# Moving one Gelu of three behind other transposes, one row's norm ahead of the next row's statistics, and twenty transposes of the identity at the start

## The chip, the cores and the metric

The kernel runs as one program on one NeuronCore of a Trainium2 chip. TensorE (PE) multiplies and transposes, VectorE (DVE) and ScalarE (ACT) read PSUM and work elementwise, GpSimd (POOL) works on SBUF and issues indirect DMAs, and SyncE (SP) issues most other DMAs. Each engine runs its own list of instructions strictly in order; a semaphore wait at the head of a list holds up everything behind it. The metric is the device time of one execution in microseconds (us); the median of several executions is compared.

## The reference

Eight rows of 512 tokens of width 128 go through two layers in float32. A layer norms its input (mean and variance, no gain), and adds an attention and a feed-forward part to it.

- Layer 0: attention with 16 heads of width 64 and a causal softmax; beside it a mixture of 32 experts of which each token uses six, plus a shared expert.
- Layer 1: attention with four heads of width 32 (queries and keys normalised to length one, two key-value heads, gate on the result). Beside it three residual blocks, each of which does this:

```python
y = _qlora_linear(h, qweights[i0], ...)   # 128 -> 128
y = _layernorm(y, ln_gamma[blk], ln_beta[blk])
y = jax.nn.gelu(y, approximate=False)
y = _qlora_linear(y, qweights[i1], ...)
h = y + h
```

## The kernel before, in words

The order of all instructions on every engine is written out by hand (`manual_schedule`): the Python code calls small functions one after the other, and each call appends its instructions to the engines' lists. Nothing reorders them later.

**The start.** Eight loads bring the rows `x_0` to `x_7` on SP's queue, while ACT's queue loads the projection weights. POOL builds the identity `ident` (used as one operand of every transpose) and the masks. A row is normed by the generator `normed(b)` in four steps: (1) statistics of its four tiles on DVE (L187, L188), one `isq` on DVE (L150) and one power on POOL (`rstd`, L153); (2) four subtract-multiply instructions on DVE (`xe`, L195); (3) four transposes on PE into a PSUM bank (`tp`, L202); (4) the copy out of PSUM, `xnT`, on ACT or DVE. `ln(0, 1, 0, 0, 0)` at L1129 takes step 1 of row 0, step 1 of row 1, and then steps 2, 3, 4 of row 0. After that come the first projections (L427), the first scores (L457) and the first value projections (L438).

**Layer 0** is a loop over 193 ticks, three per pair of heads. A tick computes scores for the next third, exponentials for this one, transposes of the last one (`pt_ps`, L501) and, once per pair, the product with the values. Places in a tick (0 to 3) take side work: the deque `steps` (rest of the norms, routing, weights of layer 1; `fill` takes steps from it until a credit of DVE time is spent), the experts and the indirect gathers of the experts' results into the row (L697, on POOL).

**Layer 1** is a loop over units `u = 3 r + k`; a slot `r` is three units (k = 0, 1, 2) and works on attention row `r`, while the three feed-forward blocks n = 0, 1, 2 work on rows r + 2, r + 1 and r (`of_slot`). In unit k, `second_layer` issues: the second linear of the blocks of the last slot (`summed`, L1050; only k = 1), the output projection (`z`, k = 2), a first linear for block k (`lin_ps`, L1008), the scores of the next unit (`sc`, L915, then `neg`, L923, on DVE), this unit's exponentials on ACT (L937), `norm` of block k (squares on DVE L1024, `lin_rstd` and `yn` on POOL), the transposes and Gelu of all three blocks of the last slot (`yn_ps` L1040 on PE, L1041 on ACT; only k = 0), the product with the values (`y_ps`, k = 1), the transposes of the last unit's probabilities (`pt_ps`, L956), and the transposes of the divisors that POOL has spread out (`wide`, `tp`, L826; only k = 0). Steps of the next row's preparation (`prepared`) stand at fixed places between them. In the last slots there are no more rows for blocks 0 and 1, so that only block 2 is left in slot 8's unit 0.

PSUM has banks in three rings: two "s", two "t" and four "m". The first linear, half of layer 1's scores, `yn_ps`, `tp` and `o_ps` all take the next "m" bank, and wait until the engine that read its last content is done. `evacuate` chooses between DVE and ACT by two running sums of estimated load.

## Time and profile before

| | |
|---|---|
| median of four runs | 1172.28 us (1171.77 to 1177.32) |
| the profiled execution's own time | 1174.18 us |
| its span, first to last instruction | 1172.5 us |
| PE busy | 1082.3 us, 92% |
| DVE busy | 759.5 us, 65% |
| ACT busy | 742.0 us, 63% |
| POOL busy | 682.0 us, 58% |
| mean granted clock of PE | 0.984 |

The profile is of one execution. "Busy" is a share over stages that have different limits, so a stage must be read by itself. A timeline row gives start, duration, engine, source line, operation, what it writes and reads, and in square brackets how long the engine stood idle before it and what ended that. PEld is the loading of PE's stationary operand. The granted clock (PEclk) is 1.00 at full speed and 0.50 when PE is throttled to half; the record of the clock begins with its first event at 17.66 us, and 1.00 is shown ahead of that for want of a record.

### The profile page before, as it was taken

To read this page: it belongs to the slowest core of one execution; us is meant where nothing else is said; L and a number is where in the kernel's file an instruction comes from. 1 tells how busy PE (TensorE), PEld (TensorE's weight loads), DVE (VectorE), ACT (ScalarE), POOL (GpSimd) and SP (SyncE) were. 2 spreads that over 40 slices of the span, in tenths; PEclk is the share of its full clock that TensorE was granted. 3 is DMA by queue.
4 is the path that set the end of the run, shared out by engine and by line. 5 is a ranking of instruction groups with operands and counts; after the bars stand their busy time and mean duration, and the time that the engine had idled before them with its cause. 6 is when DMAs were issued, how large, how long until landed. Compare 5 with 4: busy or idle time off the path is not lost.

```text
span 1172.5 us, 25274 instructions
## 1 busy us (share of the span) xinstructions
PE 1082.3 (92%) x8534; PEld 727.8 (62%) x8534; DVE 759.5 (65%) x2563; ACT 742.0 (63%) x1977; POOL 682.0 (58%) x738
## 2 busy tenths in 40 slices
PE   5899999999999999999999999999995978888986
PEld 2556556566766686667676766565663555655664
DVE  4676775665566646664666566766751667778884
ACT  3478685666466646674667466646652656887785
POOL 2008888888840000288888600488888788776650
PEclk9999999999999999999999999999997998999999
DMA  9807943368875766699889864322322241000000
GB/s 287 223 2 212 264 135 101 124 180 260 235 206 160 203 175 163 168 228 205 198 198 230 198 162 117 90 26 35 74 52 30 25 97 15 10 10 10 10 20 18
DMA packets 204052, 151.05 MB, mean 129 GB/s; under 512 B 17682, under 2 KB 192276, under 8 KB 203924
## 3 DMA queue, kind: packets, MB, share of 16 engines
q1 hardware_dynamic: 166340, 119.51, 37.2%
q0 software_dynamic: 36864, 28.34, 13.0%
q10 hardware_dynamic: 720, 1.61, 0.4%
q8 instruction: 67, 1.10, 0.4%
q14 instruction: 61, 0.50, 0.1%
HBM read 93.52 MB, written 55.87 MB: 127 GB/s over the span
## 4 chain that ended last, share of the span: by engine, by line
PE 59%; POOL 18%; DVE 9%; issue 6%; DMA 4%; SPq 2%; ACT 1%; ACTq 0%; DVEq 0%; POOLq 0%
PE sc L457 10%; POOL x L697 10%; PE pt_ps L501 9%; PE yps L524 9%; PE qk_ps L427 7%; PE z L585 4%; PE v_ps L438 3%; POOL rn L153 3%; PE ye_ps L679 2%; PE u_ps L667 2%; PE g_ps L667 2%; PE xt_ps L655 2%; DMA rb<-sums 1%; DVE neg L923 1%; POOL xs L605 1%
## 5 line engine op out<-in xcount | busy, mean ns | idle before, releaser
L697 POOL DMA_INDIRECT x<-ys,index x192 | 300.6, 1565 | 276.2 <-DMA ys<-yg 149.1
L480 ACT ACTIVATE neg<-neg,nmax 128x512 f32<-128x512 f32 (+3 forms) x512 | 281.3, 554 | 22.4 <-DVE nmax L465 22.2
L465 DVE CUSTOM_DVE_ANT_0 neg<-sc,mask 128x512 f32<-128x512 f32 (+3 forms) x512 | 225.0, 486 | 93.7 <-PE sc L457 88.6
L169 ACT COPY pT<-pt_ps 128x512 f32<-128x512 f32 x283 | 155.7, 583 | 141.3 <-PE pt_ps L501 123.8
L457 PE MATMUL sc<-qkT 64*128 64x384 f32 (+3 forms) x1024 | 193.3, 465 | 21.2 <-DVE nmax L465 21.1
L605 POOL DMA_INDIRECT xs<-xe,index x192 | 187.4, 976 | 36.7 <-issue 36.2
L501 PEld LDWEIGHTS pt_ps<-ident,neg 128*128 128x128 f32 x1280 | 137.6, 141 | 74.7 <-issue 33.8
L501 PE MATMUL pt_ps<-ident,neg 128*128 128x128 f32 x1280 | 182.5, 282 | 1.3 <-DVE pT L163 1.0
L524 PEld LDWEIGHTS yps<-pT,vs 128*64 128x64 f32 x1792 | 110.5, 137 | 77.3 <-issue 22.7
L457 PEld LDWEIGHTS sc<-qkT 64*128 64x128 f32 x1024 | 87.0, 187 | 114.6 <-DVE nmax L465 36.5
L524 PE MATMUL yps<-pT,vs 128*64 128x128 f32 (+1 forms) x1792 | 153.8, 323 | 0.8 <-ACT pT L169 0.8
L480 ACT ACTIVATION_READ_ACCUMULATOR neg<-neg,nmax 128x1 f32 x512 | 97.8, 191 | 0.0
L163 DVE COPY pT<-pt_ps 128x512 f32<-128x512 f32 x117 | 76.8, 685 | 7.6 <-PE pt_ps L501 4.1
L561 DVE TENSOR_TENSOR yT<-yT,rb 128x512 f32<-128x512 f32 x64 | 46.4, 732 | 49.2 <-DMA rb<-sums 49.1
L169 ACT COPY yT<-yps 128x512 f32<-128x512 f32 x42 | 24.6, 586 | 80.3 <-PE yps L524 80.3
L937 ACT ACTIVATE neg<-neg,nmax 128x512 f32<-128x512 f32 (+3 forms) x128 | 70.2, 552 | 0.1
L427 PE MATMUL qk_ps<-xnT,wk_sb 128*128 128x512 f32 x128 | 68.4, 617 | 0.0
L427 PE MATMUL qk_ps<-xnT,wq_sb 128*128 128x512 f32 x128 | 67.2, 607 | 0.8 <-ACT xnT L169 0.7
L438 PE MATMUL v_ps<-wv_sb,xnT 128*128 128x512 f32 x128 | 65.4, 596 | 0.0
L585 PE MATMUL z<-wz_sb,yT 128*128 128x128 f32 x512 | 63.5, 276 | 1.4 <-DVE yT L561 1.0
L585 PEld LDWEIGHTS z<-wz_sb,yT 128*128 128x128 f32 x512 | 60.5, 192 | 5.0 <-issue 2.1
L153 POOL TENSOR_TENSOR lin_rstd<-isq,neg_half 128x4 f32<-128x4 f32 x24 | 26.9, 1120 | 61.2 <-DVE isq L150 48.8
(198 smaller groups left out, 1706.4 us busy)
## 6 DMA issues: line engine op xcount, KB each, us to landing
wx<-in_experts SPq DMA_DIRECT2D x256, 128.0 KB
xs<-zero SPq DMA_DIRECT2D x16, 1280.0 KB
xg<-xs SPq DMA_DIRECT2D x64, 320.0 KB
rb<-sums SPq DMA_DIRECT2D x128, 128.0 KB
ys<-yg SPq DMA_DIRECT2D x32, 512.0 KB
oh<-slot_rows SPq DMA_DIRECT2D x32, 128.0 KB
xs<-xe,index POOLq DMA_INDIRECT x192
x<-ys,index POOLq DMA_INDIRECT x192
```

Of the source, the lines that this page charges most:

```text
L163: nc.vector.tensor_copy(dst, src)
L169: nc.scalar.copy(dst, src)
L427: nc.tensor.matmul(ps, lhsT=w[:, c * P : (c + 1) * P], rhs=xnT[b], start=True, stop=True)
L438: nc.tensor.matmul(ps, lhsT=xnT[b][:, t * P : (t + 1) * P], rhs=wv[:, g * 512 : (g + 1) * 512], start=True, stop=True,)
L457: nc.tensor.matmul(sc[j][:, off : off + w], lhsT=qT[r, i * P : (i + 1) * P], rhs=kT[r, :w], start=True, stop=True,)
L465: nc.vector.tensor_tensor_reduce(out=neg[:, j, off : off + w], in0=sc[j][:, off : off + w], in1=mask[:, L - w :], scale=-1.0, scalar=HUGE, ...
L480: nc.scalar.activation(neg[:, j, off : off + w], neg[:, j, off : off + w], AF.Exp, bias=nmax[:, 2 * k + j : 2 * k + j + 1], scale=-1.0, ac ...
L501: nc.tensor.transpose(ps[:, (start + k) * P : (start + k + 1) * P], pr[:, j, k * P : (k + 1) * P], ident,)
L524: nc.tensor.matmul(y[j * DK0 : (j + 1) * DK0, i * P : (i + hi - lo) * P], lhsT=vs[:, k, h * DK0 : (h + 1) * DK0], rhs=pt[:, j, lo:hi, :].r ...
L585: nc.tensor.matmul(z[:, t, :], lhsT=yts[b * NPAIR + c][:, (NT - 1 - t) * P : (NT - t) * P], rhs=wz[:, c, :], start=(c == 0), stop=False,)
L605: move = nc.gpsimd.indirect_dma_start(xs[h], bass.IndirectOffsetOnAxis(index[:, t, k : k + 1], 0), xe[h][:, t % TH, :], None,).ins
L697: nc.gpsimd.indirect_dma_start(x_b[b][:, tb, :], None, ys[t // TH], bass.IndirectOffsetOnAxis(index[:, t, k : k + 1], 0), compute_op=ALU.add,)
```

## The change

1. In unit k = 0 of a slot, the transposes and the Gelu of block 2 are no longer issued with those of blocks 0 and 1, but behind the transposes of the probabilities and of the divisors. This concerns eight slots (rows 0 to 7 of block 2). Around it, on ACT, the copies of the probabilities and the divisors now come ahead of that Gelu, and since the Gelu's estimated load is added later, `evacuate` gives a few copies to the other engine.
2. At the start row 0 goes through all its steps before row 1's statistics are taken. In the deque the steps of rows 1 to 3 are ordered anew to fit: row 1's second step comes ahead of row 2's statistics; the logits of the router (L223) come one half tick earlier on PE, ahead of a scores group.
3. Ahead of all that PE does twenty transposes of `ident` into a bank of its own, whose content nobody reads.

The instructions of POOL and SP stay as they are, in number and in order; PE gets the twenty transposes, and ACT and DVE the same work with a few copies exchanged.

```diff
     steps = deque(
-        ln(2, 1, 3, 1, 1, 2, 2, 2, 3, 3, 3) + [routes[0]] * 8 + [scaled] + [routes[0]] * 13
+        ln(1, 2, 1, 1, 3, 2, 2, 2, 3, 3, 3) + [routes[0]] * 8 + [scaled] + [routes[0]] * 13
...
         job(new, norm, *item)
         if k == 0:
             for old in of_slot(r - 1):
-                job(True, gelu, *old)
+                job(old[0] < 2, gelu, *old)
         job(k == 1 and past, values1, r - 1)
         advance(1)
         job(0 <= u - 1 < 3 * B, transposes1, *divmod(u - 1, 3))
         job(k == 0 and past, spread1, r - 1)
+        if k == 0:
+            for old in of_slot(r - 1):
+                job(old[0] == 2, gelu, *old)
         job(k == 2 and past, stored, r - 1)
...
-    for step in ln(0, 1, 0, 0, 0):
+    warm = bank("m", "warm")
+    for _ in range(20):
+        nc.tensor.transpose(warm[:, :P], ident, ident)
+    for step in ln(0, 0, 0, 0, 1):
         take(step)
```

## The prediction

> **What bounds the kernel now.** I read the chain of waits on the page first, then the timeline of the first 60 us, then the granted clock by stretches, then the timeline of every place in layer 1 where block 2's transposes stand.

> ```profile
> PE 59%; POOL 18%; DVE 9%; issue 6%; DMA 4%; SPq 2%; ACT 1%; ACTq 0%; DVEq 0%; POOLq 0%
> ```

> The chain is PE's, but for short stretches, from 13 to about 760 us. From there to 994 us the gathers on POOL set the pace, and they start when the ticks of layer 0 allow it. So a start that comes earlier carries through to 994 us; POOL and SP keep their order. From 994 us on DVE, POOL and PE take turns. The start:

> ```profile
> 7.14 0.17 DVE L150 TENSOR_SCALAR isq<-mv 128x4 f32<-128x4 f32 x1
> ...
> 7.40 1.05 POOL L153 TENSOR_TENSOR rstd<-isq,neg_half 128x4 f32<-128x4 f32 x1 [3.37 <-DVE isq L150]
> 9.21 0.29 DVE L187 BATCH_NORM_STATS2 bn<-x 128x6 f32<-128x128 f32 x1 [1.90 <-DMA x<-in_x]
> ...
> 11.01 1.11 DVE L195 TENSOR_SCALAR xe<-x,mv,rstd 128x128 f32<-128x128 f32 x4
> ...
> 13.33 2.08 PE L427 MATMUL qk_ps<-xnT,wq_sb 128*128 128x512 f32 x2 [0.67 <-ACT xnT L169]
> ...
> 16.91 1.41 PE L427 MATMUL qk_ps<-xnT,wq_sb 128*128 128x512 f32 x2
> ```

> Row 0's `rstd` is ready at 8.45, but `xe` stands behind row 1's statistics, which wait for row 1's load until 9.21. The first projections take 1.87 and 1.71 us from start to start, against 0.86 later: PE is at half speed here, until 17.66. The clock by stretches (columns: stretch, length, busy PE, PEld, DVE, ACT, POOL, then granted clock, DMA share, GB/s):

> ```profile
> 14.25:17.66 3.41, 3.41 (x5) 1.35 (x4) 0.69 (x1) 0.51 (x1) 0.00 (x0) 1.00 1.14 355
> 51.79:55.21 3.42, 1.13 (x6) 0.71 (x7) 3.35 (x21) 2.31 (x6) 0.00 (x0) 1.00 0.48 130
> 55.21:58.62 3.41, 3.41 (x11) 1.73 (x8) 3.19 (x31) 1.02 (x3) 0.13 (x1) 0.50 0.00 0
> 898.30:901.71 3.41, 3.20 (x11) 2.30 (x12) 1.55 (x7) 1.52 (x4) 2.99 (x2) 0.50 0.16 19
> 901.71:905.12 3.41, 3.41 (x11) 1.43 (x11) 1.38 (x7) 0.58 (x1) 2.92 (x2) 0.50 0.35 43
> ```

> ```profile
> 1040.44 0.63 PE L1040 MATMUL yn_ps<-ident,yn 128*128 128x128 f32 x4 [1.43 <-DVE nmax L923]
> ...
> 1042.24 0.17 DVE L150 TENSOR_SCALAR isq<-lin_s 128x4 f32<-128x4 f32 x1
> ...
> 1042.49 1.02 POOL L153 TENSOR_TENSOR lin_rstd<-isq,neg_half 128x4 f32<-128x4 f32 x1 [3.30 <-DVE isq L150]
> ```

> Block 2's transposes wait 1.43 us for a bank, which DVE frees by reading scores. But DVE has no gap from 1035.0 to 1047.7, and what follows is POOL: `lin_rstd`, `yn`, `rn` to 1048.75, then DVE again. The wait is PE's alone. The last slot:

> ```profile
> 1158.73 0.66 PE L1040 MATMUL yn_ps<-ident,yn 128*128 128x128 f32 x4 [0.56 <-POOL yn L1031]
> 1158.98 0.24 DVE L969 RECIPROCAL rinv<-ssum 128x16 f32<-128x16 f32 x1
> ...
> 1159.36 0.61 POOL L971 COPY wide<-rinv 128x512 f32<-128x512 f32 x1 [0.68 <-DVE rinv L969]
> 1159.46 1.28 ACT L1041 ACT_TABLE_LOAD   x1 [2.43 <-PE yn_ps L1040]
> 1160.10 0.60 PE L826 MATMUL tp<-ident,wide 128*128 128x128 f32 x4
> ...
> 1161.59 1.13 PE L1050 MATMUL o_ps<-yn,wT 128*128 128x512 f32 x2 [0.89 <-ACT yn L1041]
> ```

> Here everything hangs on block 2's Gelu: its transposes, the table load and Gelu (to 1161.54), `o_ps`, the values, the end. The divisors' `tp` can start only at 1160.0.

> **The change part by part.**

> *Row 0 first.* `xe` can start at 8.45 + 0.05 = 8.50 and ends 9.61 (1.11 as now). The last transpose ends at about 9.93 (0.04 + 0.28), the copy at 10.57 (0.58 + 0.06 of gaps), the first projection starts at 10.6 instead of 13.33: -2.7. Its weights landed by 7.15, the keys' by 11.45 at the latest (SP's load that waits for their lane was issued then); they are needed at about 12.4. Row 1's statistics (1.9) follow at 9.6 to 11.5 and lie ahead of the first `qkT` copy, which can't start before 12.4: hidden, as long as PE is at half speed; at full speed the copy would wait 0.1.

> *The clock.* In the profiled run PE's unbroken work began at 13.33 and full speed came 4.33 later, so half of that, 2.2 us, was lost. From 10.6 on the clock comes back 3.41 to 6.83 later, as the grid falls: 1.7 to 3.4 lost, 2.6 in the middle: +0.4 against this run.

> *Twenty transposes.* At half speed eight transposes took 1.70 us from start to start (980.23 to 981.93), 0.21 each; twenty from 1.4 us, when `ident` is there, end at about 5.7. PE has nothing else until 8.9, so they cost nothing; they would cost if each took over 0.37. Gain: between 0 and -2.5 (the 2.2 lost above and 0.3 of the first `tp`). I take 0. To wake the clock a stretch of the grid must lie wholly in 4.25 us, which holds for (4.25 - 3.41) / 3.41 = 25% of positions, and then 3.2 us without work follow: the row at 51.79 lost the clock with a gap of 3.06.

> [...]

> *Rows 1 to 3 in new order.* The same DVE instructions between 25 and 35 us; one copy of `vs` (0.69) comes onto DVE, one `qkT` and one `pT` leave it. The logits (3.69 on PE) run ahead of 0.63 of scores instead of behind. PE then waits for DVE anyway (3.06 at 54.08). I take +0.2, with ends -0.6 (one `tp` that no longer stands in the way) and +0.9 (0.44 of transposes behind a wait, 0.4 of scores). Start in all: -2.7 + 0.4 + 0.2 = -2.1.

> *Block 2's Gelu, slots 1 to 5* (979 to 1097 us). PE fills its 1.43 with the probabilities' transposes (0.87), waits for the same bank with `tp`, then does `yn_ps`: `o_ps` starts about 0.5 earlier. ACT loses its gap of 0.39 and starts the exponentials 0.2 earlier. DVE and POOL, on which the slot hangs, wait for none of it: 0. Ends: -1.43 for each of five, -7.2, if PE did bind; +0.6 each, one ACT copy ahead of the Gelu, +3.0.

> *Slot 6* (1121.58, waited 1.30): from here the chain is PE's to 1139. `o_ps` starts at 1122.7 instead of 1123.36: -0.6.

> *Slot 7* (1142.54). `tp` waits for `wide` until 1143.03, `yn_ps` follows to 1144.1. On ACT the table load ends at 1143.46; then one Gelu (0.73), two `pT` copies and `rT` (0.55 each), and only then the second Gelu, done at 1146.6 instead of 1144.9. `o_ps` of block 2 ends 1.2 later. ACT's exponentials, 0.7 late, and the values' 1.2 catch up in the waits for `pT`: z starts 0.8 late. +0.8.

> *Slot 8* (the fence above). The probabilities' transposes go first, then PE waits for `wide` (1159.97) with `tp` at 1160.0, and `yn_ps` runs 1160.5 to 1161.1 instead of 1158.73 to 1159.40. The table load stands behind it as now: +1.7 on everything behind. What is late next is `o_ps`, the values, the end; nothing covers it.

> End in all: -0.6 + 0.8 + 1.7 = +1.9. Sum: -2.1 + 1.9 = -0.2, on the profiled execution's 1174.18: 1174.0. The median stands 1.9 below that execution, so the forecast of the median is 1172.28 - 0.2 = 1172.1.

> **The rivals.** 0.5% of the median, 5.9 us, is about what a measurement of this kernel can tell from no change.

> *The clock does hold* until the first row arrives: 1172.1 - 2.5 = 1169.6. For it: at half speed the transposes might take longer than 0.21 and so fill the gap. Against: the gap of 3.06.

> *PE binds in slots 1 to 5 after all*, and each gives back up to 1.43: 1172.1 - 7.2 = 1165 at most, with the clock 1162.5. For it: the chain of waits runs through `yn_ps` and `tp` into `lin_rstd` in four of these slots. Against: `lin_rstd` starts 0.08 after `isq` there, and PE's `tp` ends at the same moment only because both started from the same `nmax`.

> *Slower: the divisors hold up the last slot and the start's gain is lost.* If routing on DVE (9.52 us busy of the 10 from 50 to 60) takes back what the start gains, the end's +1.9 stays, and the time is 1172.28 + 1.9 = 1174.2. It decides wherever the start brings less than 1.9. It takes half-speed stretches besides to pass 1178: a slot with one took 30.1 us (1042.5 to 1072.6) against 26.75 without, and three more would do.

> **How the numbers follow.** My forecast 0.55 (own range 1169.9 to 1174.3: the ends of the start's and the last slots' terms), the clock holds 0.15, slots 1 to 5 give back 0.18, slower 0.12. The lower end of the range goes to 1165.8, most of the second rival; the upper one to 1176.0, the third and one half-speed stretch. Faster by over 0.5% (below 1166.4) needs most of what slots 1 to 5 could give, or less of it with the clock: 0.16 of the 0.18 and 0.02 of the clock's 0.15, 0.18. Slower by over 0.5%: half of the third rival, 0.06. Between: 0.76.

> **What would show it.** Right: `xe` of row 0 at about 8.5, first projection at 10.6, its start-to-start still 1.7 or more; PE idle 3 us ahead of row 0's transposes; slots 1 to 5 with the same 26.7 to 30 us; the last `yn_ps` behind `tp`, ACT's table load 2.3 to 2.8 before `o_ps`. Wrong: projections of 0.86 at 10.6 (the clock held); slots shorter by over a microsecond; a last stretch from `fin` to the end that is not longer.

## The result and the profile after

The changed kernel takes 1178.53 us (median of 42 runs, 1171.02 to 1184.47), the kernel before 1174.87 us (median of 63 runs, 1171.23 to 1181.29). The ratio is 1.0027, with a 95% interval of 1.0017 to 1.0037: 3.2 us more (2.0 to 4.3). That is under the half per cent named as the least that can be told from no change, but the interval leaves zero out, so the change costs a little. The forecast was 1172.1, in a range of 1165.8 to 1176.0. Of the miss of 6.4 us, 2.6 lie in the base: four runs gave 1172.28, and 63 give 1174.87. The rest, 3.8, is the change, which was put at -0.2 and came out at +3.7 by the medians.

The profiled execution took 1178.42 us (its span 1176.7, mean granted clock 0.973; before: 1174.18, 1172.5 and 0.984). The chain of waits on the page after:

```profile
PE 67%; POOL 16%; DVE 7%; issue 5%; ACT 2%; DMA 2%; SPq 1%; ACTq 0%; POOLq 0%; DVEq 0%
```

PE's share was 59% before. Eight points of the span are some 94 us, far more than what was added, so the share says only that more of this chain runs through PE. The start, from PE's timeline of the changed kernel (start, length, then what it waited for):

```profile
1.42 4.07 PE L1134 MATMUL warm<-ident 128*128 128x128 f32 x20 [1.42 <-POOL ident masks.py:199]
8.91 1.24 PE L202 MATMUL tp<-ident,xe 128*128 128x128 f32 x4 [3.42 <-DVE xe L195]
10.83 2.07 PE L427 MATMUL qk_ps<-xnT,wq_sb 128*128 128x512 f32 x2 [0.68 <-ACT xnT L169]
12.70 1.91 PE L427 MATMUL qk_ps<-xnT,wk_sb 128*128 128x512 f32 x2
```

This is as forecast: the first projection comes 2.5 us earlier than at 13.33, PE is idle for 3.42 us ahead of row 0's transposes, and the first two groups are 1.87 apart, so they run at half speed. Later in the same timeline the gain goes:

```profile
30.49 1.10 PE L202 MATMUL tp<-ident,xe 128*128 128x128 f32 x4 [1.74 <-DVE xe L195]
...
32.50 2.08 PE L457 MATMUL sc<-qkT 64*128 64x384 f32 x8
36.60 1.15 PE L202 MATMUL tp<-ident,xe 128*128 128x128 f32 x4 [2.02 <-DVE xe L195]
```

The same three groups before:

```profile
33.62 1.10 PE L202 MATMUL tp<-ident,xe 128*128 128x128 f32 x4 [1.04 <-DVE xe L195]
34.65 1.14 PE L457 MATMUL sc<-qkT 64*128 64x384 f32 x8
...
37.71 1.10 PE L202 MATMUL tp<-ident,xe 128*128 128x128 f32 x4 [1.34 <-DVE xe L195]
```

The first `tp` in each is row 2's and the other row 3's. Before, they waited 1.04 and 1.34, and the eight `sc` took 1.14 us. Here the waits are 1.74 and 2.02, and `sc` takes 2.08. The clock by stretches says why (columns as in the prediction: busy PE is the second number, the granted clock stands ahead of the last two):

```profile
25.40:28.82 3.42, 3.18 (x14) 1.43 (x12) 3.18 (x17) 2.69 (x8) 1.01 (x1) 1.00 1.01 269
28.82:32.23 3.41, 1.74 (x6) 0.78 (x6) 2.38 (x9) 0.61 (x2) 1.01 (x1) 0.99 1.02 267
32.23:35.64 3.41, 2.35 (x9) 1.19 (x8) 0.91 (x3) 2.48 (x6) 0.00 (x0) 0.50 1.03 273
35.64:39.06 3.42, 2.46 (x9) 2.01 (x10) 1.58 (x10) 0.42 (x1) 0.00 (x0) 0.50 1.01 269
39.06:42.47 3.41, 3.41 (x14) 1.28 (x14) 0.00 (x0) 1.24 (x3) 0.00 (x0) 0.51 1.02 269
```

The stretch with the wait is busy 51%, and the three that follow run at half speed; before, the clock was full from 17.66 to 55.21. An instruction that started 2.5 us earlier than before at 29 us starts 0.8 us later at 60 us. The last slot, from the timeline and the stretches of the changed kernel:

```profile
1159.86 0.66 PE L826 MATMUL tp<-ident,wide 128*128 128x128 f32 x4 [0.84 <-POOL wide L971]
1160.35 0.60 PE L1040 MATMUL yn_ps<-ident,yn 128*128 128x128 f32 x4
...
1161.02 1.28 ACT L1041 ACT_TABLE_LOAD   x1 [1.38 <-PE yn_ps L1040]
1162.31 0.78 ACT L1041 ACTIVATE yn<-yn_ps,beta_sb,gamma_sb 128x512 f32<-128x512 f32 x1
...
1163.14 2.08 PE L1050 MATMUL o_ps<-yn,wT 128*128 128x512 f32 x2 [2.20 <-ACT yn L1041]
...
1165.15 4.16 PE L984 MATMUL y_ps<-pT,qkv 128*32 128x384 f32 x40
...
1170.13 1.16 PE L998 MATMUL z<-wo_sb,yT 128*128 128x128 f32 x8 [0.82 <-DVE yT L992]
```

```profile
1158.63:1162.04 3.41, 1.48 (x12) 1.00 (x10) 1.12 (x3) 2.03 (x3) 0.61 (x1) 0.99 0.27 77
1162.04:1165.46 3.42, 2.32 (x6) 0.70 (x10) 0.20 (x1) 1.04 (x2) 0.00 (x0) 0.50 0.00 0
1165.46:1168.87 3.41, 3.41 (x32) 1.28 (x28) 0.55 (x1) 0.00 (x0) 0.00 (x0) 0.51 0.00 0
```

Before, the values' product and the last `z` were:

```profile
1162.64 2.37 PE L984 MATMUL y_ps<-pT,qkv 128*32 128x384 f32 x40
...
1165.89 1.16 PE L998 MATMUL z<-wo_sb,yT 128*128 128x128 f32 x8 [0.88 <-DVE yT L992]
```

`yn_ps` starts 1.6 us later than at 1158.73, as forecast. But PE now waits 2.20 us for the Gelu where it waited 0.89, the stretch is busy 43%, and the clock drops for the next two: `o_ps` takes 2.08 instead of 1.13, the product with the values behind it 4.16 instead of 2.37, and the last `z` starts 4.2 us late, not 1.7.

### The profile page after: what moved, and what is told of

Same layout as the page of the kernel before. It is cut to its first block, busy times and chain, and to the rows that moved or that the text cites. A ratio compares the mean times of both kernels' runs of the same rounds, so it can differ in the third digit from the quotient of the medians.

```text
span 1176.7 us, 25307 instructions
## 1 busy us (share of the span) xinstructions
PE 1093.2 (93%) x8554; PEld 732.0 (62%) x8554; DVE 758.2 (64%) x2563; ACT 742.5 (63%) x1977; POOL 683.2 (58%) x738
## 3 DMA queue, kind: packets, MB, share of 16 engines
q1 hardware_dynamic: 166340, 119.51, 36.9%
## 4 chain that ended last, share of the span: by engine, by line
PE 67%; POOL 16%; DVE 7%; issue 5%; ACT 2%; DMA 2%; SPq 1%; ACTq 0%; POOLq 0%; DVEq 0%
PE sc L457 11%; PE pt_ps L501 11%; PE yps L524 10%; POOL x L697 10%; PE qk_ps L427 8%; PE v_ps L438 4%; PE z L585 4%; PE ye_ps L679 3%; PE g_ps L667 2%; PE u_ps L667 2%; PE xt_ps L655 2%; POOL rn L153 2%; PE pt_ps L956 1%; DMA xg<-xs 1%; PE sc L915 1%
## 5 line engine op out<-in xcount | busy, mean ns | idle before, releaser
L480 ACT ACTIVATE neg<-neg,nmax 128x512 f32<-128x512 f32 (+3 forms) x512 | 281.3, 554 | 23.6 <-DVE nmax L465 23.3
L169 ACT COPY pT<-pt_ps 128x512 f32<-128x512 f32 x285 | 156.9, 584 | 142.4 <-PE pt_ps L501 124.7
L457 PEld LDWEIGHTS sc<-qkT 64*128 64x128 f32 x1024 | 87.3, 188 | 114.1 <-DVE nmax L465 34.8
L480 ACT ACTIVATION_READ_ACCUMULATOR neg<-neg,nmax 128x1 f32 x512 | 97.8, 191 | 0.0
L169 ACT COPY yT<-yps 128x512 f32<-128x512 f32 x42 | 24.6, 587 | 80.5 <-PE yps L524 78.7
L427 PE MATMUL qk_ps<-xnT,wk_sb 128*128 128x512 f32 x128 | 69.1, 623 | 0.0
L427 PE MATMUL qk_ps<-xnT,wq_sb 128*128 128x512 f32 x128 | 67.3, 607 | 0.8 <-ACT xnT L169 0.7
L153 POOL TENSOR_TENSOR lin_rstd<-isq,neg_half 128x4 f32<-128x4 f32 x24 | 26.9, 1120 | 62.4 <-DVE isq L150 50.5
```

What stands on the lines that cost most here:

```text
L169: nc.scalar.copy(dst, src)
L427: nc.tensor.matmul(ps, lhsT=w[:, c * P : (c + 1) * P], rhs=xnT[b], start=True, stop=True)
L457: nc.tensor.matmul(sc[j][:, off : off + w], lhsT=qT[r, i * P : (i + 1) * P], rhs=kT[r, :w], start=True, stop=True,)
L480: nc.scalar.activation(neg[:, j, off : off + w], neg[:, j, off : off + w], AF.Exp, bias=nmax[:, 2 * k + j : 2 * k + j + 1], scale=-1.0, ac ...
```

## Two lengths to compare by

Single executions of one kernel spread by 10 us, and a profile is one of them. Two lengths in a profile don't depend on what lies between: **the early way**, from the first projection (`qk_ps`) to the 41st matmul of layer 0's scores (`sc`), and **the last way**, from the start of the last single `lin_ps` matmul to the last row's first `z`. Before, they are 54.94 - 13.33 = 41.61 us and 1165.89 - 1153.93 = 11.96 us; after, 44.94 and 16.37. All profiles:

| kernel | rows 1 to 3 | first projection | early way | half speed within 17 to 48 us | last way | whole time against before, us |
|---|---|---|---|---|---|---|
| before | old | 13.33 | 41.61 | none | 11.96 | |
| after | new | 10.83 | 44.94 | 32.2-42.5 | 16.37 | +3.2 (2.0 to 4.3) |
| e1 | old | 13.41 | 44.47 | 39.8-43.2 | 15.30 | +3.5 (2.0 to 5.1) |
| e2 | new | 10.95 | 44.80 | 32.0-42.2 | 11.96 | -2.0 (-4.0 to 0.1) |
| e3 | old | 13.31 | 41.32 | none | 11.96 | +0.7 (-1.1 to 2.5) |
| e4 | new | 11.20 | 44.10 | 31.4-34.8, 38.3-41.7 | 11.96 | -0.1 (-2.4 to 2.0) |
| e5 | new | 10.95 | 44.13 | 31.1-34.5, 37.9-41.3 | 13.62 | -2.2 (-5.0 to 0.6) |
| e6 | old | 11.04 | 44.49 | 37.5-40.9 | 11.96 | -5.9 (-8.5 to -3.2) |
| e7 | old | 10.96 | 41.18 | none | 11.96 | -4.3 (-7.4 to -1.3) |
| e8 (= after) | new | 11.18 | 44.12 | 37.2-40.6 | 13.62 | +0.7 (-1.7 to 2.9) |
| e9 | new, filled | 10.67 | 40.98 | none | 11.97 | -1.5 (-3.9 to 0.8) |
| e10 (= e5) | new | 10.61 | 44.14 | 37.2-40.6 | 13.62 | +2.1 (-1.3 to 5.6) |
| e11 (= e6) | old | 10.88 | 43.44 | 43.2-50.0 | 11.96 | -2.2 (-4.7 to 0.3) |
| e12 (= e7) | old | 10.97 | 42.78 | 42.4-49.2 | 11.97 | -2.1 (-4.6 to 0.3) |
| e13 | new, filled | 10.80 | 40.35 | 41.0-47.9 | 13.62 | +2.2 (0.8 to 3.6) |
| e14 | new, filled | 10.80 | 40.31 | 41.2-48.1 | 11.96 | -2.0 (-3.9 to 0.0) |
| e15 (= after) | new | 11.03 | 44.08 | 36.9-40.3 | 16.66 | +3.3 (1.2 to 5.3) |
| e16 | new, filled | 10.85 | 39.79 | none | 11.96 | -1.7 (-4.0 to 0.8) |
| e17 (= e7) | old | 10.77 | 41.20 | 40.4-47.2 | 11.97 | 0.0 (-2.6 to 2.6) |

The last column is the measured ratio with its 95% interval, times the median of the kernel before in the same set. "Filled" is explained with e9.

Runs e1 to e4 and e13 to e15 were on chips (11 and 8 by their record) where the kernel before takes 1176 us. Runs e5 to e12 and e16, e17 were on two others (2 and 15), where it takes 1391 to 1395 us. The profiles from there show some 220 us more between 100 and 410 us: PE is busy 144 us of these 310 (e8: 55.3, 55.3 and 33.4 in three parts), where it was busy 306 before (98.7, 97.8, 109.1). The gains of the start have to pass through that, so from these sets I use the two ways, and the whole times only with reserve. Some of the expectations call it one slower chip and a wait for transfers; the longest of PE's waits there (15.0 and 19.3 us in e6) end on nothing that the profile shows, so its cause is open.

## The experiments

**The parts alone (e1 to e4).** My theory after the result was that the loss is in the last slot; the rival, that the start's new order costs.

e1, the Gelu's move alone:

```diff
-                job(True, gelu, *old)
+                job(old[0] < 2, gelu, *old)
@@ behind job(k == 0 and past, spread1, r - 1)
+        if k == 0:
+            for old in of_slot(r - 1):
+                job(old[0] == 2, gelu, *old)
```

> Only the move of the third block's transposes and Gelu; the start is as before. Theory (the loss is in the last slot: 1.7 us for the Gelu that comes later, 2.6 us for TensorE that drops to half its clock after the longer pause): 3 to 5 us above before, with yn_ps, o_ps, y_ps and yT of the last slot shifted by 1.6 and then 4.2 us against those of before, and a granted clock of half from about o_ps to yT. Rival (the loss is in the new order of the start, which the later waits hid in part): within 1.5 us of before, and the last slot's yT no more than 1.8 us later against z of the slot before.

e2, the start's order alone:

```diff
-        ln(2, 1, 3, 1, 1, 2, 2, 2, 3, 3, 3) + ...
+        ln(1, 2, 1, 1, 3, 2, 2, 2, 3, 3, 3) + ...
-    for step in ln(0, 1, 0, 0, 0):
+    for step in ln(0, 0, 0, 0, 1):
```

> Only row 0's norm ahead and the new order of rows 1 to 3; no warm transposes, and the Gelu as before. Theory (the loss is at the end): row 0's first projection at 10.8 us instead of 13.3, and 0.5 to 2.5 us below before at the end, the less the more of 29 to 47 us runs at half clock, as it did with the change in full (there the gain of 2.5 us was turned into a loss of 0.8 us by 47 us). Rival (the start's order costs): 1 to 3 us above before, with the shift against before at 47 us at +0.8 or more.

e3, the warm transposes alone:

```diff
+    warm = bank("m", "warm")
+    for _ in range(20):
+        nc.tensor.transpose(warm[:, :P], ident, ident)
     for step in ln(0, 1, 0, 0, 0):
```

> Only the 20 warm transposes, with every order as before. Their result is read by nobody. Theory: within 0.7 us of before: they end at 5.5 us, the clock that they wake is lost before the first projection, and that starts at 13.3 us as before. Rival (the transposes shift the grid of the clock so that 29 to 47 us fall into half clock): 1 to 4 us above before, with half clock between 30 and 45 us, where before had it in full.

e4, the whole change with the Gelu at its old place in the last two slots:

```diff
-                job(old[0] < 2, gelu, *old)
+                job(old[0] < 2 or r > 6, gelu, *old)
...
-                job(old[0] == 2, gelu, *old)
+                job(old[0] == 2 and r <= 6, gelu, *old)
```

> The whole change, save that the third block's transposes and Gelu stay at their old place in the last two slots (they move in slots 1 to 6 alone). Theory (the last two slots hold the loss): 3 to 6 us below the changed kernel, so 0 to 2.5 us below before; no half clock between yn_ps and yT of the last slot. Rival (the start or slots 1 to 6 hold the loss): 2 to 4 us above before, as the changed kernel.

e1 came out at +3.5, the whole of the loss; e2 at -2.0, e3 at +0.7, e4 at -0.1, each where the theory had it. So the rival falls on whole times: no cost of the start alone is seen, and the Gelu's move in the last two slots costs. But e2's profile also has the loss of 31 to 42 us (first projection 2.4 us earlier, the 41st `sc` 0.8 later than before). In e1 the last slot shows the wait without the first half-speed stretch:

```profile
1165.72 0.60 PE L1040 MATMUL yn_ps<-ident,yn 128*128 128x128 f32 x4
1168.51 1.12 PE L1050 MATMUL o_ps<-yn,wT 128*128 128x512 f32 x2 [2.20 <-ACT yn L1041]
1169.57 4.04 PE L984 MATMUL y_ps<-pT,qkv 128*32 128x384 f32 x40
```

The wait is the same 2.20, `o_ps` is at full speed, and only the values' product is slow: the half-speed stretch begins 10.5 us after `lin_ps`, where it began 8.2 after it in the profile after. The seven distances between the first `z` of one row and the next, from the traces, show what the Gelu does slot by slot:

| kernel | 1 | 2 | 3 | 4 | 5 (slot 6) | 6 (slot 7) | 7 (slot 8) |
|---|---|---|---|---|---|---|---|
| before | 29.77 | 27.96 | 30.10 | 24.88 | 23.93 | 18.97 | 13.63 |
| e1, moved everywhere | 29.82 | 27.96 | 30.10 | 24.86 | 23.35 | 19.79 | 16.97 |
| e4, moved to slot 6 | 29.24 | 29.57 | 28.48 | 26.47 | 23.34 | 18.97 | 13.63 |
| after | 29.35 | 29.58 | 28.49 | 26.48 | 23.35 | 19.79 | 18.05 |
| e8 (= after) | 29.17 | 29.57 | 28.49 | 26.48 | 23.34 | 19.79 | 15.29 |
| e17, not moved | 29.22 | 29.57 | 28.50 | 26.49 | 23.93 | 18.97 | 13.64 |

The move is worth 0 in the first four columns, and in slot 1 ahead of them, where it is 39.85 us from layer 0's last `z` to layer 1's first in both (e1 against before; e17, without the move, has the same pattern as e4 with it, which follows the place of the half-speed stretches: before, one from 1055.3 to 1058.7 in the third column; after, from 1025.5 to 1028.9 in the second and from 1083.5 to 1086.9 in the fourth), -0.58 in slot 6, +0.82 in slot 7 and +1.66 in slot 8. On top of the last come 0 (e8), 1.68 (e1), 2.76 (after) and 3.05 (e15) us of half speed, by how the pause falls on the grid.

**Is it the wait or the clock? (e5 to e12)** e5 is the changed kernel with PE kept busy while it waits for the last Gelu:

```diff
+    def keep_busy():
+        ps = bank("m", "busy")
+        for _ in range(18):
+            nc.tensor.transpose(ps[:, :P], ident, ident)
...
                 job(old[0] == 2, gelu, *old)
+            job(r == B, keep_busy)
```

> The whole change, and 18 more transposes of the identity in the last slot, behind yn_ps, into a bank that nobody reads; they fill 1.9 of the 2.2 us that TensorE waits for the last Gelu. Theory (the wait of 1.6 us costs 1.5 to 2.6 us more because the pause drops TensorE's clock): no half clock from yn_ps to yT of the last slot, o_ps 1.1 and y_ps 2.4 us long as before the change, and 1.3 to 2.6 us below the changed kernel, so 0.5 to 2 us above before. Rival (the wait alone is the loss, or the clock is lost whatever TensorE does): 2.5 to 4 us above before.

e6 is the kernel before with row 0's norm first, and rows 1 to 3 in their old order:

```diff
-    for step in ln(0, 1, 0, 0, 0):
+    for step in ln(0, 0, 0, 0, 1):
```

> Before, with row 0's norm whole ahead of row 1's statistics, and rows 1 to 3 in their old order. Theory (the new order of rows 1 to 3 makes TensorE wait 1.7 us for row 2's xe, and that pause drops the clock in 32 to 42 us): the shift against before is -2.5 us until 29 us and still -2 or lower at 54 us, with no half clock in 30 to 42 us; 1.5 to 2.5 us below before at the end. Rival (the earlier start meets something that the later part needs anyway, whatever the order of rows 1 to 3): -2.5 until 29 us, and between -0.5 and +1 at 54 us; within 1 us of before at the end.

e7 is e6 with a longer warm-up:

```diff
+    warm = bank("m", "warm")
+    for _ in range(44):
+        nc.tensor.transpose(warm[:, :P], ident, ident)
     for step in ln(0, 0, 0, 0, 1):
```

> The same as the kernel with row 0's norm ahead and rows 1 to 3 in their old order, and 44 transposes of the identity at the start, which nobody reads, in place of none: TensorE is busy from 1.4 to about 8 us, instead of to 5.5 us as with the 20 of the change. Theory (20 wake the clock and then lose it in the 3.4 us without work; 44 hold it): full clock from 5 us on through row 0's first projections, which take 1 us less each, and 1.5 to 2.5 us below the kernel without them, so 3 to 5 us below before. Rival (the clock is lost all the same in row 0's norm, or the transposes hold up row 0's): within 1 us of the kernel without them.

e8 is the changed kernel again:

> The changed kernel as it is, beside the others on the same chip: 2 to 5 us above before by the first measurement, with row 2's wait of 1.7 us at 30 us and half clock in 32 to 42 us, and half clock in one or two stretches of 3.41 us between yn_ps and yT of the last slot.

e5 has no half speed in the last slot, and so takes 13.62 us for the last way; but e8, with nothing to fill the pause, took 13.62 as well, so this pair tells nothing. The stretch with its wait:

```profile
1378.63:1382.04 3.41, 1.70 (x13) 1.23 (x12) 1.35 (x3) 1.95 (x3) 0.72 (x2) 1.00 0.27 77
1382.04:1385.45 3.41, 2.08 (x18) 0.74 (x22) 0.75 (x1) 1.26 (x2) 0.00 (x0) 1.00 0.00 0
```

Busy 50%, it kept the clock, while the stretch from 28.82 in the profile after, busy 51%, lost it. e6 missed my expectation: the old order lost a stretch of the clock too (37.5 to 40.9), and by 54 us the early start was used up, as the rival had it. e7 kept it there, 2.8 us ahead of before from 20 to 96 us. So the old order isn't safe, and the clean profile of before was one of the better executions. The whole times of this set were largely misses: e5 was to lie 0.5 to 2 us above before and e8 2 to 5, with half speed in its last slot; e6 gave -5.9 where I had 1.5 to 2.5 below; only e7's -4.3 is as expected, and it was to lie below e6.

The second set on chip 2 repeats three of them, and adds e9, the start's order of e2 with PE kept busy in the two waits for rows 2 and 3 ("filled"):

```diff
         yield 0.0
+        if b in (2, 3):
+            busy = bank("m", "busy")
+            for _ in range(12):
+                nc.tensor.transpose(busy[:, :P], ident, ident)
         ps = bank("m", "tp")
```

> The start of the change without the warm transposes and with the Gelu at its old place, and 12 more transposes of the identity, read by nobody, ahead of row 2's tp and 12 ahead of row 3's, where TensorE waits 1.7 and 2.0 us for xe. In the profiles so far it takes 41.2 to 41.6 us from the first projection to the 41st score matmul in the old order of rows 1 to 3 where the clock holds and 44.5 where it lost a stretch, and 44.1 to 44.9 in the new order, with half clock in 31 to 42 us each time. Theory (the waits drop the clock): no half clock in 30 to 42 us, 41.5 to 43 us for that way, and 1 to 3 us below before. Rival (the new order itself takes as long, its waits and not the clock): 43.5 to 45 us for that way at full clock, and within 1 us of before.

The other three are e5, e6 and e7 once more:

> The changed kernel with 18 transposes of the identity behind the last yn_ps, as in the run on the slower chip. In the last slot it is 11.96 us from lin_ps to z with the Gelu at its old place, and with the Gelu moved 13.62, 13.62, 15.30 and 16.37 us in four profiles. Theory (the moved Gelu costs 1.66 us always, and 0, 1.7 or 2.7 us more by how the pause falls on the clock's stretches; busy, it costs 1.66 alone): 13.6 us, no half clock, and 0.5 to 2.5 us above before, against 3.2 us for the change. Rival (the clock is lost whatever TensorE does): 15 to 16.5 us, and 3 to 4 us above before.

> Row 0's norm ahead of row 1's statistics with rows 1 to 3 in their old order, nothing else, as in the run on the slower chip, where a wait of some 200 us for transfers in 100 to 410 us lay over it. Theory (the old order keeps more of the 2.5 us, for the clock is lost in some executions only): 1 to 3 us below before. Rival (nothing is kept): within 0.7 us of before.

> The same with 44 transposes of the identity at the start. Theory (TensorE kept busy from 1.4 to 8 us holds the clock through row 0's projections; on the slower chip the way from the first projection to the 41st score matmul took 41.2 us with it and 44.5 us without): 3 to 5 us below before and 1 to 2 us below the kernel without them. Rival (what they gain was the chance fall of the clock's stretches): the same as without them, to 0.7 us.

e9 settles the place of the early loss. Its timeline and stretches at the two waits:

```profile
27.91 1.47 PE L203 MATMUL busy<-ident 128*128 128x128 f32 x12
29.81 1.10 PE L206 MATMUL tp<-ident,xe 128*128 128x128 f32 x4 [0.43 <-DVE xe L195]
30.75 1.02 PE L431 MATMUL qk_ps<-xnT,wq_sb 128*128 128x512 f32 x2
31.70 1.14 PE L461 MATMUL sc<-qkT 64*128 64x384 f32 x8
32.77 1.53 PE L203 MATMUL busy<-ident 128*128 128x128 f32 x12
34.86 1.00 PE L206 MATMUL tp<-ident,xe 128*128 128x128 f32 x4 [0.56 <-DVE xe L195]
```

```profile
27.58:30.99 3.41, 2.98 (x22) 2.35 (x21) 2.88 (x12) 1.08 (x2) 1.01 (x1) 1.00 1.03 273
30.99:34.40 3.41, 3.31 (x22) 1.98 (x20) 1.41 (x9) 2.49 (x6) 0.00 (x0) 1.00 1.02 267
```

The order is e2's, work that nobody reads is added, `xe` still comes when DVE gets to it, and yet the early way takes 40.98 us, against 44.1 to 44.9 in the seven profiles with the new order unfilled. The clock is full and `sc` takes 1.14 again. So it isn't the wait for `xe` that costs 3 us, but the speed of what follows it. The whole time hardly shows it (-1.5, -3.9 to 0.8). The repeats of e6 and e7 came out level in whole time (-2.2 and -2.1), so e6's -5.9 did not come again, and the 3 to 5 us that e12 was to gain did not show. e10 repeats e5's last way:

```profile
1384.90 0.60 PE L1040 MATMUL yn_ps<-ident,yn 128*128 128x128 f32 x4
1385.34 2.13 PE L1059 MATMUL busy<-ident 128*128 128x128 f32 x18
1387.70 1.13 PE L1050 MATMUL o_ps<-yn,wT 128*128 128x512 f32 x2 [0.23 <-ACT yn L1041]
1388.76 2.37 PE L984 MATMUL y_ps<-pT,qkv 128*32 128x384 f32 x40
```

**Does it add up? (e13 to e17)** e13 is the changed kernel with all three pauses filled (e5's, e9's, and 44 warm transposes in place of 20). e14 is e9 with the 44 warm transposes ahead, and every Gelu at its old place.

> The changed kernel with TensorE busy in its three pauses: 44 transposes of the identity at the start in place of 20, 12 each ahead of row 2's and row 3's tp, 18 behind the last yn_ps, all read by nobody. Theory (beyond the 1.66 us in the last slot, the loss is the clock): first projection at 11 us, 41 to 41.5 us from there to the 41st score matmul, 13.6 us from lin_ps to z in the last slot; 2.4 us gained by the earlier start, 0 to 3 by the held clock, 1.66 lost: 1 to 3 us below before, and 4 to 6 below the changed kernel. Rival (something else holds the loss): within 1.5 us of the changed kernel.

> The same start with its pauses filled, and every Gelu at its old place. Theory: 1.66 us below the kernel with all three pauses filled, so 2.5 to 5 us below before; 41 to 41.5 us from the first projection to the 41st score matmul and 11.96 us from lin_ps to z. Rival (the start is hidden by later waits for transfers): within 1 us of before, though the 41st score matmul comes 3 us earlier.

> The changed kernel as it is, on the chip of these runs: 3 us above before, with 44 to 45 us from the first projection to the 41st score matmul and 13.6 to 16.4 us from lin_ps to z. The rival of the first two runs would have it level with them.

The ways came out as expected or within 0.7 us of it: 40.35 and 13.62 us in e13, 40.31 and 11.96 in e14, 44.08 and 16.66 in e15. With the filled pause the last way has been 13.62 in three profiles of three, without it 13.62, 15.30, 16.37 and 16.66. The clock was not held throughout, though. The table has half speed for 6.8 us, beginning between 40 and 44 us, in e11 to e14 and e17, and no pause stands ahead of it. In e13:

```profile
37.94 4.26 PE L227 MATMUL lg<-wr_sb,xnT 128*128 128x32 f32 x32
```

```profile
37.60:41.02 3.42, 3.42 (x36) 3.25 (x32) 0.00 (x0) 2.56 (x9) 0.00 (x0) 1.00 1.02 271
41.02:44.43 3.41, 3.41 (x17) 2.69 (x17) 0.93 (x5) 0.00 (x0) 0.00 (x0) 0.50 1.02 270
```

PE was busy for the whole stretch ahead of the loss, 3.08 us of it with the router's logits, 32 matmuls with an output only 32 wide. In these five profiles the logits fill 2.51 to 3.29 us of one stretch of the grid; in the other 14 no stretch at this place has more than 2.43 us of them, and the clock held. So in these profiles the loss goes with how the logits fall on the grid. That is read from the traces; no run varied it.

The whole times did not follow the ways. e13 was to lie 4 to 6 us below the changed kernel and lies 1.1 below (+2.2 against +3.3, each to 1.5 or 2 us). That expectation left out slots 6 and 7, but they make only 0.24 together. The two profiles misled more: e13's is of its fastest execution (1174.47, the median is 1177.40) and e15's of its second slowest (1182.88, the median is 1178.66). And the start's gain does not last. In e14's profile PE is 5.6 us ahead of before from 60 to 90 us, 3.5 from 200 to 250, 2.3 at 270, and 0.1 at 300, and PE's waits between 60 and 420 us are longer there than before. From the groups of waits, before and then e14:

```profile
PE xt_ps L655 <- DMA xg<-xs: 1.2, 3, 0.4
...
PE g_ps L667 <- DMA wx<-in_experts: 0.7, 1, 0.7
```

```profile
PE xt_ps L659 <- DMA xg<-xs: 2.1, 3, 1.1
PE g_ps L671 <- DMA wx<-in_experts: 1.6, 2, 1.0
```

1.8 us go back into waits for the experts' inputs and weights. Another 2.2 us go between 113 and 124 us: there the clock is at half from 112.9 to 119.7, again after a stretch that PE filled, 3.05 us of it with the next row's logits. The prediction had said that an earlier start carries through to 994 us; in part it does not.

The last set was to tell whether the winning parts make a faster kernel: e16 is e14 with e4's rule for the Gelu (moved in slots 1 to 6 alone), e17 is e7 again.

> The start of the change with its pauses filled (44 transposes of the identity at the start, 12 each ahead of row 2's and row 3's tp, read by nobody), and the third block's transposes and Gelu moved in slots 1 to 6 alone. Theory: the 2.0 us of the filled start and 0.58 us of slot 6: 2 to 4 us below before, 23.3 us for the slot that took 23.9, 18.97 and 13.63 for the last two as before. Rival (the start's gain is taken up by waits for transfers): within 1 us of before.

> Row 0's norm ahead, rows 1 to 3 in their old order, 44 transposes of the identity at the start that nobody reads, every Gelu at its old place. Theory: 41 to 43 us from the first projection, at 10.9 us, to the 41st score matmul, and 1.5 to 4 us below before. Rival as above: within 1 us of before.

On chip 15 both intervals hold zero. The profile of e16 has the shortest early way of all (39.79), 23.35 us for slot 6 and 18.97 and 13.64 for the last two, as expected; a gain in the whole time is not shown. The best that was measured where the kernel before takes 1176 us is e14, 1173.83 us against 1175.84 (0.9983, 0.9967 to 1.0000).

## Why the prediction was wrong, step by step

- **Row 0 first, -2.7: nearly right.** The first projection starts at 10.6 to 11.2 us in seven profiles of the new order (mean 10.96) against 13.31 to 13.41 in three of the old start (mean 13.35): -2.4.
- **Twenty transposes, 0: right in the sum, wrong in its reason.** e3 measured +0.7 (-1.1 to 2.5). I gave them 25% to wake the clock, from the reading that a stretch must be busy throughout. They woke it in five of seven profiles, after stretches busy 84 to 100% (2.87 of 3.41 us in e10, 3.41 in after), and not after one of 79% (e4) or of 68% (e5). Each time it was lost again 3.4 us later, in the idle stretch before row 0, so the money was right. With 44 the first scores come 2.77 us after the first projection instead of 4.3 to 5.4, in four profiles of six; so the rival in which the clock holds would have needed a longer warm-up.
- **Rows 1 to 3 in new order, +0.2, and the clock, +0.4: the first step that failed, by the profiles.** The early way takes 44.33 us in the mean of seven profiles in the new order, against 42.47 in the mean of the three with the old start: +1.9 in place of the two terms' 0.6. I had priced the instructions that change place and the waits that they make; the end that I gave, +0.9, was for waits and scores at full speed. What a pause does to the clock of the next 3.41 us I had read off the row at 51.79, and used for the first transposes only. The clock's own +0.4 was no loss: full speed came 3.0 to 6.1 us after the first projection in the seven (mean 4.5, against 4.33 before). Nor is the new order shown to be the cause, for e6 and e11 keep the old one and took 44.49 and 43.44. The start in all is then -2.4 + 1.9 = -0.5 by the ways, not -2.1. The whole times can't tell the two apart: e2 alone measured -2.0 (-4.0 to 0.1), and e4, with the transposes and slot 6's gain, -0.1 (-2.4 to 2.0).
- **Slots 1 to 5, 0; slot 6, -0.6; slot 7, +0.8: right**, at 0, -0.58 and +0.82. PE did not bind there, so the second rival falls.
- **Slot 8, +1.7: the delay and its size were right, the step ended too early. This is the failure that whole times show:** e1 alone measured +3.5 (2.0 to 5.1), where the terms of slots 6 to 8 make +1.9. Where the clock held (e5, e8, e10, e13) the last way is 13.62 us, 1.66 more than before. "Nothing covers it" was true, and it was not all: PE's pause grew from 0.89 to 2.20 us, and behind it stand `o_ps` and the values' product, PE work of 3.4 us at full speed, which ran at half speed, wholly or in part, in three of four profiles. In the mean of the four that is 0 + 1.68 + 2.76 + 3.05 over 4 = 1.9 us more.
- **The sum.** -0.5 for the start, +1.9 for slots 6 to 8, +1.9 for the clock in slot 8: +3.3, against the +3.2 measured. That it agrees so well is partly luck: the start's term rests on ways of single executions, with a mean of only three on one side, and e2's whole time gives -2.0 for it. Also, e13 and e14 differ by 4.2 us (1.8 to 6.6) where slots 6 to 8 explain 1.9.
- **The slower rival** said that the start's gain is lost and the end's +1.9 stays. The time is near that, but the early way was lost by the clock (40.98 us in e9, where it held, against 44.94 in the profile after) and not by routing on DVE, and it needed no "three more" stretches in slots to get to 1178: the two behind the last Gelu and the base were enough.
- **The base** was the median of four runs, where one profiled execution already stood 1.9 above it. A median over more runs lay 2.6 higher.

The clock's grid does not lie at the same place in every run. For the same changed kernel one of its edges is at 4.92 us in the profile after, at 6.19 in e15 and at 6.47 in e8, and the last slot lost 2.76, 3.05 and 0 us to half speed. I had allowed for any place of the grid in the first 10 us, and took the rest of the profile as fixed.

What stays open: at which activity a stretch keeps the clock (the busy time in the profile does not tell it, see below), how much of a start's gain survives layer 0's transfers and logits, and what held chips 2 and 15.

## What to carry to other kernels

A change that lengthens a wait of TensorE by one or two microseconds should be priced with what stands behind the wait, at half speed: here a delay of 1.66 us cost 1.66 in every profile and up to 3.05 more. Put the pause on the clock's grid at several positions and take the mean, and see whether work that nobody needs can fill it (with 18 transposes the clock held in three profiles of three, without them in one of four). And before a sum is set against a profile, ask whether that execution was a lucky one: two lengths taken from several profiles told more here than the whole times, which spread by 10 us.

## What I had not expected of the hardware

- The clock's loss does not follow the busy share of the stretch before it. It was lost, among others, after 1.09, 1.21, 1.39, 1.48, 1.68 and 1.74 us of 3.41, and twice after 2.07 (e1 and e6, just before 39.77 and 37.49), but kept after 1.47 (e10, 98.65 to 102.06), after 1.70 (e8) and after 2.07 in the profile before (34.73 to 38.14). And it was lost after 3.41 of 3.41, where the logits with their 32-wide outputs filled 2.51 to 3.29 us of the stretch (e11 to e14, e17).
- Transposes of a constant that nobody reads count as work for the clock. The trace lists them as MATMUL; 20 of them raised it to full in five profiles of seven (from 4.92 us in the profile after; before, the first on record is at 17.66), and with 12 or 18 it held at full in every pause that they filled (1.00 from 27.58 to 34.40 us in e9 and from 1378.99 to 1389.22 in e10).
- Chips 8 and 11 ran the same kernel before at 1176 us, chips 2 and 15 at 1391 to 1395, with TensorE's mean granted clock at 0.98 and 0.90. All of the difference lies between 100 and 412 us, by the changed kernel's profiles of e8 and after: 219 us behind at 412 us, and 218 at the end.
